# PixArt block on one core: nine narrow zero matmuls at the beginning, and each unit's third-next source transposed whole in beat 0, the turned maxima in a PSUM bank of their own

## The chip, the cores and the metric

One core of one Trainium2 chip. The metric is the time of one execution on the device in microseconds, the median of three runs. A profiled execution has a time of its own; its span runs from the first to the last profiled instruction.

## The reference

A PixArt transformer block for 16 batch items of 256 tokens, width 256, 16 heads of 16 values, in fp32: modulated self-attention, cross-attention to a context of 256 rows, and an MLP of width 1024. Cut to what matters:

```python
c_proj = jax.nn.silu(c) @ W_mod + b_mod
shift_a, scale_a, gate_a, shift_m, scale_m, gate_m = jnp.split(c_proj, 6, axis=-1)
x_norm = modulate(_ln(x), shift_a, scale_a)          # t * (1 + scale) + shift
q, k, v = jnp.split(x_norm @ W_qkv + b_qkv, 3, axis=-1)
attn_w = softmax(einsum('bhqd,bhkd->bhqk', q, k) * scale)
x = x + gate_a[:, None] * (einsum('bhqk,bhkd->bhqd', attn_w, v) @ W_proj + b_proj)
q_c = _ln(x) @ W_qc + b_qc
k_c, v_c = jnp.split(_ln(context) @ W_kvc + b_kvc, 2, axis=-1)
x = x + softmax(q_c k_c * scale) v_c @ W_cproj + b_cproj
x_norm2 = modulate(_ln(x), shift_m, scale_m)
x = x + gate_m[:, None] * (gelu(x_norm2 @ W_mlp1 + b_mlp1) @ W_mlp2 + b_mlp2)
```

## The kernel before

**Units and beats.** An attention of one kind (`s` self, `c` cross) for one batch item is a unit; there are 32, in the order s0 to s4, then alternately a new `s` and the `c` of an item whose `s` is done. The main loop calls `beat(n, k)` for n = -1 to 31 and k = 0 to 7. In a beat TensorE makes one eighth of the scores of the next unit (`s`, 4 matmuls, `s_tile`), one eighth of the transposed scores of this unit (`st`, 4 matmuls, `t_part`), and then something else: in even beats the weighted values of a finished quarter (`o`, 16 matmuls, `av_part`), in odd beats projections of coming units (`lanes`). VectorE takes the row maxima `mx` of each `s`, ScalarE the exponential `pt` of each `st`. After a beat all of `s` and `st` is written anew, so the next beat's `s` follows `mx` and its `st` follows `pt`.

**What a coming unit needs.** GpSimd normalises the source of unit n+4 in beat 4 or 5 of unit n and sets `ready`. One unit later it is unit n+3 (`q3` in `beat`): TensorE transposes it (`turn`, four transposes: two halves `f` of the width, each of two row tiles) into the PSUM tile `psT`, ScalarE and VectorE split it in beat 3 into a high and a low part (`xTh`, `xTl`), and K, V and Q follow by matmuls in beats 5, 7 and 1. K of the next but one unit ends in beat 7; in the next beat 0 ScalarE copies its high part (`h_k`, or `h_kc` for a cross unit), and VectorE, after this beat's `mx`, makes the low part (`l_k`, `l_kc`), each in two instructions, the last to read the tile `ps_k`.

**The turned maxima.** Half of a unit's row maxima are turned by one transpose in beat 4 of the unit before, half in beat 0 of its own (`m_turn`); ScalarE copies them negated (`m_row`) and a DMA puts them in as a further row of Q.

**PSUM.** Two double banks are held by `s` and `st`. One bank has the tag `gen` (LONG), and three have the tag `tr` (SHORT): `psT`, `ps_k`, `ps_q`, `o`, the maxima (`psm`) and others pass through these three. A new tile of a tag waits until a bank of the tag is released, that is, until all readers of its last tile are done.

**Order.** The text of the program sets the order on each engine (`InOrder`), so an engine that waits holds up all behind it. The beginning is a list of words, `PRE` in `E_` (line 55): `b9` is `busy(9, ...)`, nine matmuls of zeros into `s`; `brow` and `turn` transpose the biases and the conditioning (`c_sb`); `scale`, `shift` and `bq`, `bk`, `bv` are small matmuls; `T0t` transposes the first source; `Q0x0`, `Q0y0`, `Q0s0` send the first head group's parts of Q of unit 0 to their places by DMA from SP's queue, and a word ending in `0a` would use ScalarE's.

Of the kernel before, what the change touches and what calls it, by code (L numbers as in the profile page):

```python
# [16 lines left out]
P = 128  # L17
# [4 lines left out]
def pixart_block(  # L22
# [8 lines left out]
    B, N, H = x.shape  # L31
# [20 lines left out]
                return tc.keep_in_program_order(i) if self.on else i  # L52
            return issue

    E_ = {'M': ((-46, -37, -26, -24, -20, -20, -18), (-26, -17, -10, -8, 1, 1, 1), (-3, 1, 4, 7, 9, 9, 9), (8, 11, 13, 15)), 'LN': {'s': 'pool', 'c': 'pool', 'q': 'pool'}, 'ON': (1, 1, 1), 'H': (7, 11, 14, 15), 'AP': 23, 'DV': (1, 2), 'E': (-14, -6, -2, 2), 'HP': (1, 0, 2), 'W1P': [(-9, 3), (-8, 3), (-7, 3), (-6, 3), (-4, 5), (-4, 7), (-3, 1), (-3, 5)], 'W2P': [(-4, 3), (-4, 7), (-3, 2), (-3, 4), (-3, 6), (-3, 7), (-2, 0), (-2, 2), (-2, 4), (-2, 6), (-1, 0)], 'PRE': 'z0qp z0kp load ld2 ld3 rest L0a L0b silu b9 brow turn b1 L0f scale hik lok T0t shift b1 T0h T0l hiq one0a loq hiv bk K0a K0m L1a L1n lov L2a L2b bq K0h K0x K0y L1e K0l K0s Q0a Q0m Q0h Q0x0 Q0y0 T1t Q0l Q0s0 Q0r ldm T1h V0a V0b z1qa T1l bv L2c z1kp L3a L3b L3p L3c K1a K1b', 'SL': {(-1, 0): 'Q1a Q1b K1x K1y K1l K1s', (-1, 1): 'T2t T2h T2p V1a Q1x Q1y Q1l Q1s', (-1, 2): 'V1b rest', (-1, 3): 'rest z2ka', (-1, 4): 'M0 rest one1 ld4', (-1, 5): 'K2a vone', (-1, 6): 'K2m z2qa', (-1, 7): 'cpm2 c1 one2', (0, 0): 'cpm0 rest', (0, 1): 'rest', (0, 4): 'rest', (1, 0): 'rest', (1, 2): 'rest', (1, 4): 'rest'}}

    PE = InOrder(nc.tensor, True)
    ACT, DVE, POOL, SP = (InOrder(e, True) for e in (nc.scalar, nc.vector, nc.gpsimd, nc.sync))
# [122 lines left out]
    def busy(n, where):  # L181

        for _ in range(n):
            PE.matmul(where[:, :N], zw[:, :P], zw, start=True, stop=True)

    ts = [work.tile([P, 2, KC, H], F32, tag="pt", name=f"wf{i}", bufs=5) for i in range(3)]
    wm0, wm1, wk, wq, wv = (ts[i // 2][:, i % 2] for i in range(5))
# [540 lines left out]
    def m_turn(u, hf, pst=None):  # L728

        if pst is None:  # L730
            pst = ps_gen(f"psm_{u.n}_{hf}", SHORT)
        PE.transpose(pst[:16, :P], u.mx[:, hf].rearrange("p r a t -> p (r a t)"), ident)
        return pst
# [37 lines left out]
    def av_part(u, g):  # L771

        if g % 2 == 0:
            u.po = ps_gen(f"o_{u.n}_{g}", SHORT).rearrange("p (g n) -> p g n", g=2)
        for c in range(NT):
            for h in range(4):
                par, pair = h // 2, 2 * g + h % 2
                PE.matmul(u.po[h * 32:(h + 1) * 32, g % 2], u.v[:, c, par * 8 + pair], u.pt[pair][:, par, c],
                          start=(c == 0), stop=(c == NT - 1), tile_position=(0, h * 32))
        if g == 3:  # L780
            o_out(u, 1)
# [321 lines left out]
    def beat(n, k):  # L1103
        if n < 0:
            visit(n, k, (st, sp)[k % 2])
            return
        cur, prev, nxt = unit(n), unit(n - 1), unit(n + 1)
        q2, q3, q4 = (v if v and v.n >= m else None
                      for v, m in zip(map(unit, (n + 2, n + 3, n + 4)), (1, 2, 3)))
        p1, p2, p3 = (v and v.post for v in map(unit, (n - 1, n - 2, n - 3)))  # L1110
        alone = n > nu - 3
        lc = q4 if q4 and q4.kind == "c" else None
        ls = q4 if q4 and q4.kind == "s" else None
        lx = q3 if q3 and q3.kind == "c" else None
        late = lc and lc.b in (0, B - 1)
        if k == 0 and q2:
            q2.K.high()
            q2.K.send_high()
        if k == 2 and q2 and n:
            q2.V.keep()  # L1120
        if k == 4 and q2:
            q2.Q.high()
            q2.Q.send_high()
        if k == 6:
            if q2 and not n:
                q2.V.keep()
            if p2 and not alone:
                p2.end()
        kp = None
        if k == 5 and lx and n:  # L1130
            kp = lanes(q3.K, None if alone else p2)
        visit(n, k, between=kp and (lambda: run(kp, 2)))
        if k == 0:
            exps()
            if prev:
                av_part(prev, 3)
            if q3 and q3.ready:
                q3.T[0].place()
                pst = m_turn(cur, 1, q3.T[0].ps[:, N:])
                q3.T[0].turn((0,))  # L1140
            else:
                pst = m_turn(cur, 1)
            if prev:
                p1.pull_sums(1)
            m_row(cur, 1, pst)
            if q2:
                q2.K.low()
                q2.K.send_low()
            if p2:
                p2.norm()  # L1150
                p2.high()
                p2.low()
        elif k == 1:
            exps()
            run(lanes(q2 and q2.Q, q2 and n and q2.V))
            if prev:
                p1.pull_values(1)
            if lc:
                lc.ln[0].steps[0]()
            if lx:  # L1160
                if lx.b in (0, B - 1):
                    lx.ln[1].steps[0]()
                lx.ln[1].steps[1]()
                lx.ln[1].steps[2]()
        elif k == 2:
            exps()
            if cur:
                av_part(cur, 0)
            if q3:
                q3.T[0].turn((1,) if q3.ready else (0, 1))  # L1170
            if ls:
                ls.ln[0].steps[0]()
            elif prev:
                p1.recip()
                p1.spread()
            if not (q3 and q3.kind == "c"):
                spare(n)
        elif k == 3:
            if q3:
                q3.T[0].high()  # L1180
            exps()
            if q3 and q3.kind == "c" and n < nu - 4:
                q3.T[0].full()
            if alone and p2:
                p2.proj(0)
                p2.proj(1)
            elif n:
                run(lanes(p2, q2 and q2.Q))
            else:
                run(lanes(q2.V, q2.Q))  # L1190
            if q3 and q3.kind == "s":
                q3.T[0].low()
            if prev and ls:
                p1.recip()
                p1.spread()
            if lx and n == nu - 4:
                lx.T[0].parts[2]()
        elif k == 4:
            exps()
            if alone:  # L1200
                p2.end()
            if cur:
                av_part(cur, 1)
            if lx:
                lx.T[1].turn()
            if nxt:
                m_part(nxt, 0, st[:, 0] if lx else None)
            if q2:
                q2.Q.low()
                q2.Q.send_low()  # L1210
            if q3 and q3.kind == "c":
                if n < nu - 4:
                    q3.T[0].rest_pool()
                spare(n, not lc)
            if ls:
                ls.ln[0].steps[1]()
                ls.ln[0].steps[2]()
                ls.ready = True
        elif k == 5:
            exps()  # L1220
            run(kp or lanes(q3 and q3.K, (None if alone else p2) if n else q2.V))
            if cur:
                o_out(cur, 0)
            if lc:
                lc.ln[0].steps[1]()
                lc.ln[0].steps[2]()
                lc.ready = True
            if prev:
                p1.back()
            v = unit(n + 5)  # L1230
            if v and v.kind == "c":
                load(v)
        elif k == 6:
            exps()
            if lx:
                lx.T[1].high()
            if cur:
                cur.post.begin()
                av_part(cur, 2)
                cur.post.pull(0)  # L1240
            if q3 and p2:
                q3.vk = lanes(q3.V, q3.K)
                run(q3.vk, 1)
            if p3:
                p3.store()
            if lx:
                if lc:
                    p1.gate()
                    if not late:
                        lc.ln[1].steps[0]()  # L1250
        elif k == 7:
            exps()
            if lx:
                lx.T[1].parts[2]()
            run(q3.vk if q3 and p2 else lanes(q3 and q3.V, q3 and q3.K))
            if late:
                p2.add()
                p2.added = True
            elif lc and not lx:
                lc.ln[1].steps[0]()  # L1260
            v = unit(n + 5)
            if v and v.kind == "s":
                load(v)
            if n == nu - 1:
                p2.add()
                p2.store()
# [106 lines left out]
```

## Time and profile before

| | |
|---|---|
| time, median of 3 runs | 720.54 us (720.0 to 723.34) |
| profiled execution | 721.24 us, span 719.4 us |
| TensorE busy | 710.9 us, 99% of the span |
| VectorE, ScalarE, GpSimd busy | 79%, 77%, 73% |
| TensorE on the chain that ended last | 96% |

The names: PE is TensorE, PEld its weight loads, DVE VectorE, ACT ScalarE, POOL GpSimd, SP the queue that issues most DMAs. A row of the timeline has the start in us, the duration in us, the engine, the line, the operation, out<-in with the tiles' names, the shapes and a count; in brackets stands the engine's idle time before it and what ended it. All instructions are recorded by one helper and carry its line, L51, so the tile names tell them apart. A fp32 matmul that isn't of the rounded kind (`fp32r`) makes two passes on the array.

### The profile page before, as it was taken

Reading aid. Unit: us, or ns where it says so; the run is one execution under the profiler, and the core shown is the slowest. Engines: PE = TensorE matmul, PEld = TensorE weight load, DVE = VectorE, ACT = ScalarE, POOL = GpSimd, SP = SyncE. Lnnn points to the kernel's source line nnn. Section 1 sums busy time; section 2 is a strip of 40 time slices with the busy share of each in tenths; the row PEclk is TensorE's granted clock in tenths of the full one; section 3 lists DMA queues with packets and bytes.
Section 4 is the critical chain, followed back from the end, with each engine's and each line's share of the span. In section 5 each row is a group of like instructions: output and inputs, shape, how many; then the busy total and the mean of one; then the engine's idle time right before and its main releaser. Section 6 shows DMA issues by size and latency. Waiting matters only on the chain.

```text
span 719.4 us, 22486 instructions
## 1 busy us (share of the span) xinstructions
PE 710.9 (99%) x8991; PEld 591.3 (82%) x8991; DVE 565.9 (79%) x895; ACT 552.0 (77%) x955; POOL 521.7 (73%) x518
## 2 busy tenths in 40 slices
PE   9999999999999999999999999999999999999997
PEld 8777877778777787777877777787679999999997
DVE  4788888888888888888889888888765767777653
ACT  4677888888888888888888888878867677666761
POOL 6656678786866868686686788977866989666551
PEclk9999999999999999999999999999999999999999
DMA  6565445544545455454555656456322222313112
GB/s 209 193 218 185 153 163 180 179 164 166 186 139 193 157 185 187 165 180 136 196 165 188 204 171 198 148 196 195 105 73 97 76 68 80 80 55 88 53 52 74
DMA packets 81548, 106.15 MB, mean 148 GB/s; under 512 B 16610, under 2 KB 44548, under 8 KB 81444
## 3 DMA queue, kind: packets, MB, share of 16 engines
q1 hardware_dynamic: 80596, 104.43, 45.1%
q8 instruction: 71, 1.16, 0.7%
q10 hardware_dynamic: 848, 0.28, 0.2%
q14 instruction: 33, 0.27, 0.1%
HBM read 35.89 MB, written 8.98 MB: 62 GB/s over the span
## 4 chain that ended last, share of the span: by engine, by line
PE 96%; DVE 2%; issue 0%; ACT 0%; POOL 0%; ACTq 0%; POOLq 0%
PE s L51 19%; PE o L51 17%; PE st L51 16%; PE ph L51 12%; PE ps_qc L51 4%; PE ps_v_c L51 4%; PE ps_q L51 4%; PE ps_k L51 3%; PE ps_P_s L51 3%; PE ps_kc L51 3%; PE ps_v_s L51 3%; PE ps_P_c L51 2%; PE psT_c L51 2%; DVE mx L51 2%; PE psT_s L51 2%; PE psT_q L51 1%
## 5 line engine op out<-in xcount | busy, mean ns | idle before, releaser
L51 DVE TENSOR_REDUCE mx<-s 128x4 f32<-128x1024 f32 x252 | 307.9, 1222 | 72.5 <-PE s L51 68.8
L51 ACT ACTIVATE pt<-st 128x1024 f32<-128x1024 f32 x256 | 263.5, 1029 | 51.2 <-PE st L51 50.1
L51 PE MATMUL o<-pt,v 128*32 128x256 f32 x2048 | 137.0, 385 | 0.0
L51 PE MATMUL s<-big 63*128 63x256 f32 x1008 | 116.9, 306 | 1.1 <-DVE st_q L51 0.2
L51 PE MATMUL st<-big 64*128 64x256 f32 (+1 forms) x1040 | 107.6, 282 | 1.0 <-issue 0.6
L51 PE MATMUL ph<-xTh_m,wself 128*128 128x256 f32 x512 | 99.5, 280 | 0.0
L51 POOL TENSOR_TENSOR hl<-hf,hh 128x512 fp32r<-128x512 f32 x60 | 80.8, 1364 | 20.0 <-ACT hh L51 20.0
L51 PEld LDWEIGHTS s<-big 63*128 63x128 f32 x1008 | 77.3, 185 | 20.6 <-issue 7.5
L51 PEld LDWEIGHTS o<-pt,v 128*32 128x32 f32 x2048 | 53.4, 109 | 39.4 <-ACT oT L51 1.1
L51 PEld LDWEIGHTS st<-big 64*128 64x128 f32 (+1 forms) x1040 | 81.2, 186 | 3.9 <-ACT pt L51 1.5
L51 PEld LDWEIGHTS ph<-xTh_m,wself 128*128 128x128 f32 x512 | 82.0, 188 | 1.2 <-issue 0.4
L51 PE MATMUL ph<-xTl_m,wself 128*128 128x256 f32 x256 | 70.9, 277 | 0.0
L51 ACT ACTIVATE hf<-ph,bT 128x256 f32<-128x256 f32 x112 | 47.3, 476 | 21.1 <-PE ph L51 21.1
L51 ACT ACTIVATE hh<-ph,bT 128x256 fp32r<-128x256 f32 x112 | 47.3, 477 | 18.1 <-PE st L51 8.2
L51 PEld LDWEIGHTS ph<-xTl_m,wself 128*128 128x128 f32 x256 | 48.2, 188 | 0.0
L51 PE MATMUL s<-big,hh 128*128 128x256 f32 x256 | 45.2, 277 | 0.0
L51 DVE TENSOR_SCALAR xn_m<-x,mv_m,rs_m 128x256 f32<-128x256 f32 x28 | 33.5, 1236 | 14.8 <-POOL rs_m L51 14.8
L51 POOL TENSOR_SCALAR xn_q<-x,mv_q,rs_q 128x256 f32<-128x256 f32 x32 | 39.0, 1229 | 1.7
L51 POOL TENSOR_SCALAR xn_c<-c,mv_c,rs_c 128x256 f32<-128x256 f32 x32 | 39.0, 1229 | 1.7
L51 POOL TENSOR_SCALAR rs_c<-mv_c 128x2 f32<-128x2 f32 x16 | 3.7, 230 | 50.3 <-DVE mv_c L51 50.1
L51 PE MATMUL st<-big,hh 128*128 128x256 f32 x224 | 39.5, 276 | 0.0
L51 PEld LDWEIGHTS s<-big,hh 128*128 128x128 f32 x256 | 38.6, 188 | 0.0
(230 smaller groups left out, 2134.0 us busy)
## 6 DMA issues: line engine op xcount, KB each, us to landing
big<-h_k SPq DMA_DIRECT2D x32, 256.0 KB
big<-h_kc SPq DMA_DIRECT2D x32, 256.0 KB
big<-h_qc SPq DMA_DIRECT2D x32, 256.0 KB
big<-h_q SPq DMA_DIRECT2D x30, 256.0 KB
big<-l_k SPq DMA_DIRECT2D x16, 256.0 KB
g<-gd SPq DMA_DIRECT2D x16, 256.0 KB
U_s<-oT SPq DMA_DIRECT2D x32, 128.0 KB
R_s<-rd_s SPq DMA_DIRECT2D x16, 256.0 KB
```

The costliest lines, as they stand in the source:

```text
L51: i = f(*a, **k)
```

## The change

Four edits:

- `busy` multiplies zeros of 128 columns instead of 256. All its words are affected: nine at the very beginning, one before `shift`'s users, and one at the end of unit -1.
- The second word of zeros, after `turn`, is `b2` instead of `b1`: two narrow ones for one wide.
- `Q0y0` becomes `Q0y0a`: the send goes out from ScalarE's queue.
- In beat 0 of a unit with a source that is ready, the maxima get a tile `psm` of their own instead of the second half of `psT`, and the source's four transposes are all issued behind it; beat 2 then has none. Where the source is not ready (unit 0), all four stay in beat 2.

```diff
-    ... 'PRE': '... silu b9 brow turn b1 L0f scale ... Q0h Q0x0 Q0y0 T1t Q0l Q0s0 Q0r ...
+    ... 'PRE': '... silu b9 brow turn b2 L0f scale ... Q0h Q0x0 Q0y0a T1t Q0l Q0s0 Q0r ...
...
     def busy(n, where):
 
         for _ in range(n):
-            PE.matmul(where[:, :N], zw[:, :P], zw, start=True, stop=True)
+            PE.matmul(where[:, :P], zw[:, :P], zw[:, :P], start=True, stop=True)
...
             if prev:
                 av_part(prev, 3)
+            pst = m_turn(cur, 1)
             if q3 and q3.ready:
-                q3.T[0].place()
-                pst = m_turn(cur, 1, q3.T[0].ps[:, N:])
-                q3.T[0].turn((0,))
-            else:
-                pst = m_turn(cur, 1)
+                q3.T[0].turn()
             if prev:
                 p1.pull_sums(1)
             m_row(cur, 1, pst)
...
             if cur:
                 av_part(cur, 0)
-            if q3:
-                q3.T[0].turn((1,) if q3.ready else (0, 1))
+            if q3 and not q3.ready:
+                q3.T[0].turn()
```

How it moves the instructions, on TensorE, in beat 0 of unit 1, the first with a ready source; `o_2` is the end of the weighted values of unit 0, `mx` the maxima of unit 1, `xn_s` the normalised source of unit 4, `big` the Q and K of a unit, and in brackets stand the engines whose semaphores an instruction waits for. Before:

```order
L51 MATMUL psT_s_830<-ident,mx_527 16x128
L51 MATMUL psT_s_830<-ident,xn_s_692 128x128 [waits Pool_49] x2
L51 MATMUL s<-big_80 128x256 [waits DVE_49]
L51 MATMUL s<-big_80 128x256 x3
L51 MATMUL st<-big_78 128x256 [waits Activation_49]
L51 MATMUL st<-big_78 128x256 x3
L51 MATMUL ps_q_855<-xTh_s_620,wself 128x256 [waits DVE_49]
```

Now:

```order
L51 MATMUL psm_1_831<-ident,mx_528 16x128
L51 MATMUL psT_s_833<-ident,xn_s_693 128x128 [waits DVE_49,Pool_49]
L51 MATMUL psT_s_833<-ident,xn_s_693 128x128 [waits Pool_49]
L51 MATMUL psT_s_833<-ident,xn_s_693 128x128 x2
L51 MATMUL s<-big_80 128x256 x4
L51 MATMUL st<-big_78 128x256 [waits Activation_49]
L51 MATMUL st<-big_78 128x256 x3
L51 MATMUL ps_q_859<-xTh_s_621,wself 128x256 [waits Activation_49]
```

Four transposes stand where two stood. The first of them now waits for VectorE as well as for GpSimd, the `s` of beat 1 behind them has lost its wait for VectorE, and the first Q projection waits for ScalarE instead of VectorE.

On VectorE at the same place (`mx_813` are the maxima of unit 2, of which one instruction falls in beat 0 and the next in beat 1; `l_k` is the low part of K of unit 3):

```order
L51 TENSOR_REDUCE mx_528<-s 128x2x2 [waits PE_49] x3
L51 TENSOR_REDUCE mx_813<-s 128x2x2 [waits PE_49]
L51 TENSOR_SCALAR l_k_842<-ps_k_713,bqkv,h_k_805 128x256 [waits DMAHW3_49,Activation_49]
L51 TENSOR_SCALAR l_k_842<-ps_k_713,bqkv,h_k_805 128x256
L51 TENSOR_REDUCE mx_813<-s 128x2x2 [waits PE_49] x2
```

This is of the changed kernel; nothing moved here, the kernel before has the same rows under other buffer numbers.

On TensorE in beat 2 of the same unit, behind the weighted values `o`. Before:

```order
L51 MATMUL o_0_893<-pt_1_853,v_82 32x256
L51 MATMUL psT_s_830<-ident,xn_s_692 128x128 x2
L51 MATMUL s<-big_80 128x256 [waits DVE_49]
L51 MATMUL s<-big_80 128x256 x3
L51 MATMUL st<-big_78 128x256 [waits Activation_49]
```

Now:

```order
L51 MATMUL o_0_897<-pt_1_857,v_82 32x256
L51 MATMUL s<-big_80 128x256 [waits DVE_49]
L51 MATMUL s<-big_80 128x256 x3
L51 MATMUL st<-big_78 128x256 [waits Activation_49]
L51 MATMUL st<-big_78 128x256 x3
```

The two transposes are gone from here, and `s` of beat 3 follows `o` directly, with its wait for VectorE as before.

More of the change, by code (lines that the diff above doesn't have):

```diff
@@ L53, in __getattr__ @@
             return issue
-    E_ = {'M': ((-46, -37, -26, -24, -20, -20, -18), (-26, -17, -10, -8, 1, 1, 1), (-3, 1, 4, 7, 9, 9, 9), (8, 11, 13, 15)), 'LN': {'s': 'pool', 'c': 'pool', 'q': 'pool'}, 'ON': (1, 1, 1), 'H': (7, 11, 14, 15), 'AP': 23, 'DV': (1, 2), 'E': (-14, -6, -2, 2), 'HP': (1, 0, 2), 'W1P': [(-9, 3), (-8, 3), (-7, 3), (-6, 3), (-4, 5), (-4, 7), (-3, 1), (-3, 5)], 'W2P': [(-4, 3), (-4, 7), (-3, 2), (-3, 4), (-3, 6), (-3, 7), (-2, 0), (-2, 2), (-2, 4), (-2, 6), (-1, 0)], 'PRE': 'z0qp z0kp load ld2 ld3 rest L0a L0b silu b9 brow turn b1 L0f scale hik lok T0t shift b1 T0h T0l hiq one0a loq hiv bk K0a K0m L1a L1n lov L2a L2b bq K0h K0x K0y L1e K0l K0s Q0a Q0m Q0h Q0x0 Q0y0 T1t Q0l Q0s0 Q0r ldm T1h V0a V0b z1qa T1l bv L2c z1kp L3a L3b L3p L3c K1a K1b', 'SL': {(-1, 0): 'Q1a Q1b K1x K1y K1l K1s', (-1, 1): 'T2t T2h T2p V1a Q1x Q1y Q1l Q1s', (-1, 2): 'V1b rest', (-1, 3): 'rest z2ka', (-1, 4): 'M0 rest one1 ld4', (-1, 5): 'K2a vone', (-1, 6): 'K2m z2qa', (-1, 7): 'cpm2 c1 one2', (0, 0): 'cpm0 rest', (0, 1): 'rest', (0, 4): 'rest', (1, 0): 'rest', (1, 2): 'rest', (1, 4): 'rest'}}
+    E_ = {'M': ((-46, -37, -26, -24, -20, -20, -18), (-26, -17, -10, -8, 1, 1, 1), (-3, 1, 4, 7, 9, 9, 9), (8, 11, 13, 15)), 'LN': {'s': 'pool', 'c': 'pool', 'q': 'pool'}, 'ON': (1, 1, 1), 'H': (7, 11, 14, 15), 'AP': 23, 'DV': (1, 2), 'E': (-14, -6, -2, 2), 'HP': (1, 0, 2), 'W1P': [(-9, 3), (-8, 3), (-7, 3), (-6, 3), (-4, 5), (-4, 7), (-3, 1), (-3, 5)], 'W2P': [(-4, 3), (-4, 7), (-3, 2), (-3, 4), (-3, 6), (-3, 7), (-2, 0), (-2, 2), (-2, 4), (-2, 6), (-1, 0)], 'PRE': 'z0qp z0kp load ld2 ld3 rest L0a L0b silu b9 brow turn b2 L0f scale hik lok T0t shift b1 T0h T0l hiq one0a loq hiv bk K0a K0m L1a L1n lov L2a L2b bq K0h K0x K0y L1e K0l K0s Q0a Q0m Q0h Q0x0 Q0y0a T1t Q0l Q0s0 Q0r ldm T1h V0a V0b z1qa T1l bv L2c z1kp L3a L3b L3p L3c K1a K1b', 'SL': {(-1, 0): 'Q1a Q1b K1x K1y K1l K1s', (-1, 1): 'T2t T2h T2p V1a Q1x Q1y Q1l Q1s', (-1, 2): 'V1b rest', (-1, 3): 'rest z2ka', (-1, 4): 'M0 rest one1 ld4', (-1, 5): 'K2a vone', (-1, 6): 'K2m z2qa', (-1, 7): 'cpm2 c1 one2', (0, 0): 'cpm0 rest', (0, 1): 'rest', (0, 4): 'rest', (1, 0): 'rest', (1, 2): 'rest', (1, 4): 'rest'}}
     PE = InOrder(nc.tensor, True)
```

## The prediction

> **What bounds the kernel now.** I read the page first, for the engine that sets the end, then TensorE's waits, then the timeline of one unit at the beats that the change touches, then the first 21 us.
>
> ```profile
> span 719.4 us, 22486 instructions
> PE 710.9 (99%) x8991; PEld 591.3 (82%) x8991; DVE 565.9 (79%) x895; ACT 552.0 (77%) x955; POOL 521.7 (73%) x518
> PE 96%; DVE 2%; issue 0%; ACT 0%; POOL 0%; ACTq 0%; POOLq 0%
> ...
> PEld s L51 <- DVE mx L51: 5.2, 13, 0.6
> ```
>
> TensorE is busy 99% of the span and carries 96% of the chain that ended last. Its longest wait for another engine, the score matmuls `s` waiting for the row maxima `mx`, is 5.2 us in all. So time added to TensorE's stream, work or waiting, comes out at the end nearly one for one, and idle time of the others is free. The question for each edit is what it adds to or takes from that stream.
>
> The change acts in every unit whose third-next source was already normalised. In the kernel before, those are the units where the maxima are turned inside the `psT` bank:
>
> ```profile
> L51 PE MATMUL psT_s<-ident,mx x12: 276/277/278, 51.7 to 380.4; 128*16 128x128 f32 x12
> L51 PE MATMUL psT_c<-ident,mx x16: 276/277/278, 82.8 to 475.0; 128*16 128x128 f32 x16
> ```
>
> 12 + 16 = 28 units, from 51.7 to 475.0 us. Here is beat 0 of the first of them (start, duration, engine, operation; several rows of the timeline left out), and the same two instructions in the last one:
>
> ```profile
> 50.16 0.40 PE L51 MATMUL s<-big 63*128 63x256 f32 x4
> 50.36 0.85 ACT L51 ACTIVATE h_k<-ps_k,bqkv 128x256 fp32r<-128x256 f32 x2 [0.30 <-PE ps_k L51]
> 50.60 1.22 DVE L51 TENSOR_REDUCE mx<-s 128x4 f32<-128x1024 f32 x1 [0.64 <-PE s L51]
> 50.73 1.07 PE L51 MATMUL o<-pt,v 128*32 128x256 f32 x16
> 51.73 0.28 PE L51 MATMUL psT_s<-ident,mx 128*16 128x128 f32 x1
> 51.74 0.87 DVE L51 SCALAR_TENSOR_TENSOR l_k<-ps_k,bqkv,h_k 128x256 fp32r<-128x256 f32 x2
> 51.84 0.38 PE L51 MATMUL psT_s<-ident,xn_s 128*128 128x128 f32 x2
> 52.00 0.59 ACT L51 COPY oT<-o 128x512 f32<-128x512 f32 x1
> 52.15 0.51 PE L51 MATMUL s<-big 63*128 63x256 f32 x4
> ...
> 475.06 0.87 DVE L51 SCALAR_TENSOR_TENSOR l_kc<-ps_kc,bP,h_kc 128x256 fp32r<-128x256 f32 x2
> 475.16 0.38 PE L51 MATMUL psT_c<-ident,xn_c 128*128 128x128 f32 x2
> ```
>
> The reader is to see the order of events: TensorE reaches the source's transposes at 51.84, and VectorE finishes the pair `l_k` only at 51.74 + 0.87 = 52.61. At 475 us it is the same: 475.16 against 475.06 + 0.87 = 475.93. Before the change nothing ties the two together.
>
> **Beat 0: a new wait.** The short tag has three banks. At this moment one holds `o` (until the copy `oT`), one holds the K projection `ps_k` (until `l_k` has read it), and the third was free. The maxima now take the third, so the transposes must have a bank that is still in use, and the order shows which: their new wait is on VectorE, where in this beat `l_k` is the last reader of a short bank. `l_k` cannot come earlier: it stands behind `mx` (50.60 + 1.22 = 51.82), which stands behind this beat's `s`. How long TensorE takes from VectorE's end to its own start is seen in beat 4, where `s` does wait:
>
> ```profile
> 58.81 1.16 DVE L51 TENSOR_REDUCE mx<-s 128x4 f32<-128x1024 f32 x1
> 60.02 0.30 PEld L51 LDWEIGHTS s<-big 63*128 63x128 f32 x4 [0.34 <-DVE mx L51]
> 60.03 0.50 PE L51 MATMUL s<-big 63*128 63x256 f32 x4
> ```
>
> 58.81 + 1.16 = 59.97, and `s` starts at 60.03: 0.05 us. So the transposes start at 52.61 + 0.05 = 52.66 instead of 51.84, +0.82 us. Behind them on TensorE's queue stand `s` and `st` of beat 1 and the projections, with VectorE's next `mx` and ScalarE's next `pt` behind those.
>
> Four transposes run there instead of two. Unit 0 of the kernel before does four at once, right after `o`:
>
> ```profile
> 40.00 0.65 PE L51 MATMUL psT_s<-ident,xn_s 128*128 128x128 f32 x4
> ...
> 40.59 0.51 PE L51 MATMUL s<-big 63*128 63x256 f32 x4
> ```
>
> 0.59 us from the first to the next `s`; in beat 0 two take 52.15 - 51.84 = 0.31. So beat 1's `s` starts at 52.66 + 0.59 = 53.25 instead of 52.15: **+1.10 us**. Bounds: 0.77 + 0.23 = 1.00 with no signal time and only the difference between four transposes (0.59) and two (0.36, beat 2 below), both right after `o`; and 1.20 if the array, drained by the wait, costs another 0.1.
>
> [...]
>
> **Beat 2: two transposes leave.**
>
> ```profile
> 54.59 1.23 DVE L51 TENSOR_REDUCE mx<-s 128x4 f32<-128x1024 f32 x1 [0.67 <-PE s L51]
> 54.72 1.07 PE L51 MATMUL o<-pt,v 128*32 128x256 f32 x16
> 55.72 0.44 PE L51 MATMUL psT_s<-ident,xn_s 128*128 128x128 f32 x2
> 56.08 0.50 PE L51 MATMUL s<-big 63*128 63x256 f32 x4
> ```
>
> They hold TensorE from 55.72 to 56.08, 0.36 us. But the `s` behind them overwrites scores that `mx` reads until 54.59 + 1.23 = 55.82, so it can start at 55.87, not 55.72: **-0.21 us**, and -0.36 only if `mx` were no limit. The transposes' reader, the copy `xTh` in beat 3, gets its data earlier; ScalarE isn't the bound.
>
> **The maxima's own bank.** The transpose of the maxima is the same instruction in another bank and costs the same. Its reader, the copy `m`, stands behind `oT` on ScalarE (to 52.59), so an earlier release helps nobody. The first Q projection of beat 1 now takes the bank that `oT` frees at 52.59 and comes after 53.25: covered. It costs only if that cover goes.
>
> Per unit: 1.10 - 0.21 = 0.89 us, times 28 = **+24.9 us**. Bounds: 1.00 - 0.36 = 0.64, or 17.9 us; 1.20 - 0.15 = 1.05, or 29.4 us, where 0.15 leaves a little for a later `mx`.
>
> **The beginning.** Nine zero matmuls are issued as 18 passes, counted here as weight loads in two stretches, and what follows them:
>
> ```profile
> 1.17:5.17 4.00, 4.00 (x9) 3.19 (x10) 0.00 (x0) 1.00 0.79 223
> 5.17:7.20 2.03, 2.03 (x10) 1.54 (x8) 0.00 (x0) 1.00 0.96 287
> ...
> 4.29 0.41 DVE L51 SCALAR_TENSOR_TENSOR c_sb<-c_sb 16x256 f32<-16x256 f32 x1
> 5.97 0.16 DVE L51 SCALAR_TENSOR_TENSOR nb_s<-mv_s,rs_s 128x2 f32<-128x2 f32 x1 [1.27 <-POOL rs_s L51]
> 7.23 0.24 PE L51 MATMUL s<-ident,brow 32*128 32x32 f32 x1
> 7.79 0.60 ACT L51 ACTIVATE xn_s<-x,nb_s,rs_s 128x256 f32<-128x256 f32 x1
> 8.28 1.05 PE L51 MATMUL st<-sw,wf 128*128 128x128 f32 x8
> 9.17 0.60 PE L51 MATMUL psT_s<-ident,xn_s 128*128 128x128 f32 x4
> ```
>
> Ten passes take the first 4.00 us (0.40 each), eight the next 2.03 (0.25): TensorE starts slow and quickens at about 5 us, though the granted clock reads 1.00 in both. At half the columns a slow pass is 0.2 us, 18 of them 3.7 to 3.9 us, so they end at about 5.2 and the bias transpose starts there instead of 7.23, about 2 us sooner. What follows could use it: its other input `c_sb` is there at 4.70, the normalised source would be at 6.13 + 0.60 = 6.73 (ScalarE started it at 7.79 only behind copies that waited for TensorE), and the transposes of 9.17 would come at 7.2. I take **-1.9 us**. The later zeros, two narrow for one wide, are as many columns; the one narrow one before the Q bias hides behind VectorE. Bounds: 0, if weights not yet landed hold the next steps (the trace doesn't show single landings), and -2.1.
>
> [...]
>
> One send of Q's first head group moves from SP's queue to ScalarE's:
>
> ```profile
> 16.83 0.84 ACT L51 ACTIVATE xTh_s<-psT_s,sc 128x256 fp32r<-128x256 f32 x2
> 17.39 1.20 SPq L51 DMA_DIRECT2D big<-h_q  x2
> 18.68 0.54 SPq L51 DMA_DIRECT2D big<-l_q  x1
> 18.58 0.36 PE L51 MATMUL ps_k<-xTh_s,wself 128*128 128x256 f32 x1
> 20.86 0.50 PE L51 MATMUL st<-big 63*128 63x256 f32 x4 [0.62 <-issue]
> ```
>
> SP issues two sends in 1.20 us, so the third (`l_q`) goes out 0.6 earlier, and the first scores (20.86), which waited 0.62 for something the profile doesn't name, could come up to 0.6 earlier. Against that, the send stands before `xTh` on ScalarE, whose 0.6 us later end pushes K1 (18.58) by up to 0.4. Between -0.6 and +0.4 I take -0.2. The one narrow zero at the end of unit -1 saves at most 0.1.
>
> Sum: the profiled execution took 721.24 us (span 719.4 and 1.8 around it). 721.2 + 24.9 - 1.9 - 0.2 - 0.1 = 743.9. The median of the three runs, 720.54, lies 0.7 below the profiled one, so I predict **743.2 us**, 3.1% slower.
>
> **The rivals.** *Part of the wait is given back* (0.09): the added idle time lets VectorE and ScalarE get ahead, so that TensorE's later waits vanish. For: VectorE is at 79% only. Against: the waits of `s` for `mx` are loops within one beat, which a delay ahead of it shifts as a whole. If all 5.2 us went and the units cost the low bound of 17.9, it is 720.5 + 17.9 - 5.2 - 2.2 = 731; with half of that, and the units at the middle, up to 737.
>
> *Faster* (0.04): the wait is already met when TensorE gets there, because `o` or `st` in beat 0 come later than before relative to `mx`, or the bank is in fact another. It decides at 52.61: if TensorE reached the transposes 0.82 us later for another reason, the wait would cost nothing and one group of four would replace two of two: (0.31 + 0.36 - 0.59) x 28 = 2.2 us saved. With the beginning: 720.5 - 2.2 - 2.2 = 716. Against: 51.84 against 52.61 in the first unit and the same 0.77 in the last; nothing in the change moves `o`. About 0.02 more lies within 0.5%, which is about what a measurement of this kernel can tell from no change.
>
> *Dearer* (0.06): the restart after the wait costs more, or the three banks, now passed round among seven tenants a unit instead of six, add a second wait, at Q for `oT`. With 0.3 us more a unit, 8.4 us: 751 to 752. For: the wait for `oT` is new. Against: it ends 0.7 us before Q comes.
>
> *The beginning doesn't do it* (within the forecast): were the clock not opened by narrow zeros, the eight passes at 8.28 and those behind would run at half speed and eat about 1 us of the lead; 744 to 745.
>
> **How the numbers follow.** The forecast has 0.79. From the bounds its own range is 720.5 + 17.9 - 2.8 = 735.6 to 720.5 + 29.4 + 0.4 = 750.3; I write 735 to 750. That leaves out the faster case, no change, the dearer case and about half of the part given back: 0.04 + 0.02 + 0.06 + 0.05 = 0.17, so the range stays there. Faster by over 0.5%: 0.04; within: 0.02; slower: 0.94.
>
> **What would show it.** Right: in beat 0 a gap on TensorE ahead of the `psT` transposes of about 0.8 us, put down to `l_k` or `l_kc`, 28 times, some 23 us in all; beat 1's `s` about 1.1 us after where it was within the unit; in beat 2 `s` 0.05 after `mx`; the unit longer by 0.9 us; the first scores near 18.8 us. Wrong: no gap there, the transposes of beat 0 starting 0.11 us after the maxima's as before, or units of the old length.

## The result and the profile after

The changed kernel takes 744.78 us (median of six executions, 743.7 to 747.47) against 721.68 us for the kernel before, measured beside it (six executions): a ratio of 1.0326, 95% interval 1.0303 to 1.0348. It is slower by 3.3%; 743.2 was predicted.

The profiled execution took 747.47 us. The page of the changed kernel, its first rows and its chain; behind it the groups of TensorE's transposes (busy time, mean ns of one, then TensorE's idle time just before them and its releasers):

```profile
span 745.7 us, 22480 instructions
PE 714.3 (96%) x8993; PEld 594.6 (80%) x8993; DVE 569.3 (76%) x895; ACT 549.5 (74%) x955; POOL 520.4 (70%) x518
PE 63%; DVE 20%; POOL 7%; issue 6%; DMA 3%; ACT 1%; POOLq 0%; SPq 0%; ACTq 0%
```

```profile
L51 PE MATMUL psm<-ident,mx 128*16 128x128 f32 x48 | 13.3, 277 | 0.0
L51 PE MATMUL psT_s<-ident,xn_s 128*128 128x128 f32 x64 | 10.6, 290 | 8.8 <-DVE l_kc L51 4.3 <-POOL U_c L51 2.2 <-POOL xTh_ac L51 0.8
L51 PE MATMUL psT_c<-ident,xn_c 128*128 128x128 f32 x64 | 10.0, 280 | 12.0 <-DVE l_k L51 3.7 <-DVE l_kc L51 2.2 <-POOL xTh_as L51 2.2
```

TensorE works 3.4 us longer and the span is 26.3 us longer: the rest is idle time. It stands in front of the sources' transposes, 8.8 + 12.0 = 20.8 us there. Its share of the chain falls from 96% to 63%, and VectorE's rises from 2% to 20%.

The names behind the arrows need care. Only about half of the idle time is put down to `l_k` or `l_kc`; the rest goes to GpSimd's instructions. In the timeline they all look alike. Beats 0 to 3 of the first unit with a ready source, after the change (start, duration, several rows left out), and the same place in the last one:

```profile
49.95 1.23 DVE L51 TENSOR_REDUCE mx<-s 128x4 f32<-128x1024 f32 x1 [0.64 <-PE s L51]
50.08 1.07 PE L51 MATMUL o<-pt,v 128*32 128x256 f32 x16
51.08 0.28 PE L51 MATMUL psm<-ident,mx 128*16 128x128 f32 x1
51.10 0.87 DVE L51 SCALAR_TENSOR_TENSOR l_k<-ps_k,bqkv,h_k 128x256 fp32r<-128x256 f32 x2
51.35 0.59 ACT L51 COPY oT<-o 128x512 f32<-128x512 f32 x1
52.11 0.63 PE L51 MATMUL psT_s<-ident,xn_s 128*128 128x128 f32 x4 [0.75 <-DVE l_k L51]
52.67 0.51 PE L51 MATMUL s<-big 63*128 63x256 f32 x4
...
54.62 0.41 PE L51 MATMUL s<-big 63*128 63x256 f32 x4
55.08 1.23 DVE L51 TENSOR_REDUCE mx<-s 128x4 f32<-128x1024 f32 x1 [0.64 <-PE s L51]
55.20 1.07 PE L51 MATMUL o<-pt,v 128*32 128x256 f32 x16
56.36 0.51 PE L51 MATMUL s<-big 63*128 63x256 f32 x4
...
498.78 0.28 PE L51 MATMUL psm<-ident,mx 128*16 128x128 f32 x1
498.80 0.86 DVE L51 SCALAR_TENSOR_TENSOR l_kc<-ps_kc,bP,h_kc 128x256 fp32r<-128x256 f32 x2
499.81 0.63 PE L51 MATMUL psT_c<-ident,xn_c 128*128 128x128 f32 x4 [0.75 <-POOL x L51]
```

In the first unit `l_k` ends at 51.10 + 0.87 = 51.97 and the transposes start at 52.11. In the last, `l_kc` ends at 499.66 and they start at 499.81, again 0.15 later, though the row there names GpSimd's `x`. The order names VectorE as what they wait for in both, and in all 28 units the first transpose starts 147 or 148 ns after the pair `l_k` or `l_kc` ends, whatever name the row gives. So all 28 are the wait for the bank. From the maxima's transpose to the next `s` it is now 52.67 - 51.08 = 1.59 us, against 52.15 - 51.73 = 0.42 before.

From the first such unit to the last it is 498.78 - 51.08 = 447.70 us, against 475.04 - 51.73 = 423.31: 24.39 us over 27 units, **0.90 us each**. Twenty-eight make 25.3 of the 26.3 us.

The beginning, after the change (TensorE's rows; the first scores and the first product of the output at the end):

```profile
1.17 4.21 PE L51 MATMUL s<-zw 128*128 128x128 f32 x18 [1.17 <-DVE zw L51]
5.32 0.31 PE L51 MATMUL s<-ident,brow 32*128 32x32 f32 x1
5.90 1.22 PE L51 MATMUL s<-zw 128*128 128x128 f32 x4
6.92 1.92 PE L51 MATMUL st<-sw,wf 128*128 128x128 f32 x8
8.62 1.06 PE L51 MATMUL psT_s<-ident,xn_s 128*128 128x128 f32 x4
...
20.34 0.50 PE L51 MATMUL st<-big 63*128 63x256 f32 x4
38.35 1.07 PE L51 MATMUL o<-pt,v 128*32 128x256 f32 x16
```

The bias transpose starts at 5.32 instead of 7.23, the 1.9 us that were forecast. But the eight passes `st` behind it now take 1.92 us where they took 1.05, and the four transposes 1.06 where they took 0.60: slow passes. At the first `o` of the units only 39.00 - 38.35 = 0.65 us are left of the lead, in this execution.

### The profile page after: what moved, and what is told of

It reads as the page before. It is cut to its first block, busy times and chain, and to the rows that moved or that the text cites. A ratio compares the mean times of both kernels' runs of the same rounds, so it can differ in the third digit from the quotient of the medians.

```text
span 745.7 us, 22480 instructions
## 1 busy us (share of the span) xinstructions
PE 714.3 (96%) x8993; PEld 594.6 (80%) x8993; DVE 569.3 (76%) x895; ACT 549.5 (74%) x955; POOL 520.4 (70%) x518
## 3 DMA queue, kind: packets, MB, share of 16 engines
q8 instruction: 71, 1.16, 0.7%
## 4 chain that ended last, share of the span: by engine, by line
PE 63%; DVE 20%; POOL 7%; issue 6%; DMA 3%; ACT 1%; POOLq 0%; SPq 0%; ACTq 0%
PE s L51 15%; DVE mx L51 13%; PE ph L51 12%; PE st L51 11%; PE o L51 6%; PE ps_q L51 2%; PE ps_P_s L51 2%; PE ps_P_c L51 2%; PE ps_k L51 2%; DVE st_c L51 1%; PE ps_kc L51 1%; PE ps_v_s L51 1%; PE psT_s L51 1%; PE psT_c L51 1%; POOL xn_c L51 1%
```

## The experiments

My theory: in each unit TensorE stands still until `l_k` has read its bank, and that is nearly the whole loss. The rivals: four transposes at once cost it, whatever bank they have; or the beginning hides a larger loss or gain.

**The units' change alone.** The head stays as it was.

```diff
+            pst = m_turn(cur, 1)
             if q3 and q3.ready:
-                q3.T[0].place()
-                pst = m_turn(cur, 1, q3.T[0].ps[:, N:])
-                q3.T[0].turn((0,))
-            else:
-                pst = m_turn(cur, 1)
+                q3.T[0].turn()
...
-            if q3:
-                q3.T[0].turn((1,) if q3.ready else (0, 1))
+            if q3 and not q3.ready:
+                q3.T[0].turn()
```

> The kernel before with the change in the units alone (maxima in a bank of their own, all four transposes in beat 0); its beginning is that of the kernel before. Theory (a wait for l_k in each unit): in the changed kernel beat 1's s came 1.16 us later after the turned maxima than before, and beat 2 gave back some 0.25, so 28 x 0.91 = 25.5 us more than before, about 746 to 747 us, with the gap of 0.9 us in front of the transposes in 28 units. Rival (part of the loss lies in the beginning or in the end): clearly less than 24 us.

Measured: 747.76 us (745.5 to 750.2), ratio 1.0353 [1.0315, 1.0391]. The expectation was 746 to 747. In two of the four executions (749.39 and 750.2) the mean granted clock was 0.995, and the last section shows what that costs; the other two took 745.5 and 746.12, and the kernel before without such executions 721.1 in the median, so the units cost 24.7 us. The idle time in front of the sources' transposes is 9.0 + 12.0 = 21.0 us here, 0.75 a unit, where 0.9 was expected. So the units carry all of the loss, and the beginning takes a little off it.

**The beginning alone.** The units stay as they were.

```diff
-    ... 'PRE': '... silu b9 brow turn b1 L0f ... Q0x0 Q0y0 T1t ...
+    ... 'PRE': '... silu b9 brow turn b2 L0f ... Q0x0 Q0y0a T1t ...
-            PE.matmul(where[:, :N], zw[:, :P], zw, start=True, stop=True)
+            PE.matmul(where[:, :P], zw[:, :P], zw[:, :P], start=True, stop=True)
```

> The kernel before with the change at the beginning alone (narrow zeros, two for one, Q's send from ScalarE). Theory (the clock opens late after narrow zeros, as in the changed kernel's trace, where TensorE's passes stay at 0.21 us until 9.7 us): the lead of 1.9 us at the bias transpose shrinks to about 0.65 us at the first weighted values, so about 0.6 to 1.3 us under before. Rival (the late opening was an accident of that one execution, and the lead usually holds): 1.9 to 2.2 us under before, with passes of 0.11 us from about 5.3 us on.

Measured: 718.44 us (717.81 to 721.16) against 721.39 for before, ratio 0.9957 [0.9938, 0.9975]: a gain of 3.0 us, 1.8 to 4.5. That is more than either expectation gave (0.6 to 1.3, and 1.9 to 2.2). It is the fastest kernel of this study. Its profiled execution kept only 39.00 - 38.29 = 0.71 us at the first `o`, like the changed kernel's; why the time is better than that trace is taken up below, as far as it is known.

**The maxima in their own bank, the transposes still two and two.**

```diff
+            pst = m_turn(cur, 1)
             if q3 and q3.ready:
                 q3.T[0].place()
-                pst = m_turn(cur, 1, q3.T[0].ps[:, N:])
                 q3.T[0].turn((0,))
-            else:
-                pst = m_turn(cur, 1)
```

> As e1, but the transposes stay split as before, two in beat 0 and two in beat 2: only the bank of the maxima is changed. Theory (the loss is the bank, so the wait for l_k): the transposes of beat 0 wait 0.92 us more, beat 2 stays as before, 28 x 0.92 = 25.8 us more than before, about 747 us. Rival (the loss is in issuing four transposes at once in beat 0): about as before, 721 us.

Measured: 746.71 us (745.16 to 748.38), ratio 1.0338 [1.0303, 1.0374], as slow as with all four at once. Its first unit:

```profile
51.17 0.87 DVE L51 SCALAR_TENSOR_TENSOR l_k<-ps_k,bqkv,h_k 128x256 fp32r<-128x256 f32 x2
52.18 0.41 PE L51 MATMUL psT_s<-ident,xn_s 128*128 128x128 f32 x2 [0.74 <-DVE l_k L51]
52.52 0.51 PE L51 MATMUL s<-big 63*128 63x256 f32 x4
```

The same wait stands in front of two transposes. How many are issued together isn't the cause; the maxima's bank is.

**The maxima in their own bank, all four transposes in beat 2.**

```diff
-            if q3 and q3.ready:
-                q3.T[0].place()
-                pst = m_turn(cur, 1, q3.T[0].ps[:, N:])
-                q3.T[0].turn((0,))
-            else:
-                pst = m_turn(cur, 1)
+            pst = m_turn(cur, 1)
...
             if q3:
-                q3.T[0].turn((1,) if q3.ready else (0, 1))
+                q3.T[0].turn()
```

> As e1, but all four transposes are issued in beat 2, where l_k has long read its bank: the maxima have a bank of their own and the source is transposed whole. Theory (the loss is the wait alone): beat 0 loses two transposes (s 0.21 us sooner), beat 2 gets two (s 0.23 us later), so within 1.5 us of before, 720 to 723 us, and no wait for l_k. Rival (a seventh tile through three banks costs in any place): 10 us or more over before.

Measured: 728.25 us (726.41 to 729.71), ratio 1.0079 [1.0049, 1.0109]. A miss by some 5 us. The large wait is gone, as expected, but beat 0's saving comes back in beat 1. So the rival was right in kind, a further tile through three banks costs here too, though less than its 10 us. The groups of the first Q weights, for this kernel and then for the kernel before (two rows each), and one instance at 308 us:

```profile
L51 PEld LDWEIGHTS ps_q<-xTh_s,wself 64*128 64x128 f32 (+1 forms) x240 | 31.2, 190 | 2.5 <-DVE l_k L51 2.3
L51 PEld LDWEIGHTS ps_qc<-xTh_q,wqch 64*128 64x128 f32 x128 | 23.6, 185 | 3.1 <-DVE l_kc L51 3.1
```

```profile
L51 PEld LDWEIGHTS ps_q<-xTh_s,wself 64*128 64x128 f32 (+1 forms) x240 | 30.6, 185 | 0.1
L51 PEld LDWEIGHTS ps_qc<-xTh_q,wqch 64*128 64x128 f32 x128 | 23.6, 185 | 0.2 <-DVE l_kc L51 0.2
```

```profile
307.84 0.28 PE L51 MATMUL psm<-ident,mx 128*16 128x128 f32 x1
307.86 0.87 DVE L51 SCALAR_TENSOR_TENSOR l_k<-ps_k,bqkv,h_k 128x256 fp32r<-128x256 f32 x2
308.05 0.50 PE L51 MATMUL s<-big 63*128 63x256 f32 x4
308.78 0.18 PEld L51 LDWEIGHTS ps_q<-xTh_s,wself 64*128 64x128 f32 x1 [0.20 <-DVE l_k L51]
```

With the transposes gone from beat 0, `s` follows the maxima 0.21 us later instead of 0.42, and Q reaches its bank before `l_k` lets it go (307.86 + 0.87 = 308.73): 2.3 + 3.1 = 5.4 us of waits for `l_k` and `l_kc`, where the kernel before had 0.2. The bank is due at one time, and whoever asks for it first waits. (In its profiled execution, 727.9 us long, the clock was also halved for a while; that is the last section's.)

**The transposes ahead of the maxima.** The units' change alone, with the two statements of beat 0 in the other order.

```diff
-            pst = m_turn(cur, 1)
             if q3 and q3.ready:
                 q3.T[0].turn()
+            pst = m_turn(cur, 1)
```

> The units' change alone (the head as before), but with the source's four transposes written ahead of the maxima's turn in beat 0, so that the two trade the banks they are given: the transposes take the bank that came free earlier and it is now the maxima's turn that asks for the bank which `l_k` releases. Nothing is left out of the computation. Theory (the loss is TensorE standing idle until `l_k` has read its bank, and it shrinks by whatever is put in front of the waiting instruction): the four transposes, 0.56 us from their start to the first scores, now run while `l_k` is under way, and the wait of about 0.91 us shrinks to about 0.35 us in each of 28 units; 28 x 0.56 = 16 us less than the units' change alone, so about 732 us (729 to 736). Rival (the loss is four transposes in beat 0, or a wait that is as long wherever it stands): 746 to 749 us as before.

Measured: 734.27 us (733.29 to 738.92), ratio 1.0181 [1.014, 1.0221]; 13.5 us less than the units' change alone (12.3 without the executions at a mean clock of 0.995), where the theory said 16 and the rival nothing. The theory had taken a wait of 0.91 us, of which the trace shows 0.75 as idle time. The wait has moved to the maxima's transpose. What is left of it, as a group and in the first unit:

```profile
L51 PE MATMUL psm<-ident,mx 128*16 128x128 f32 x48 | 13.3, 277 | 7.8 <-DVE l_kc L51 4.2 <-DVE l_k L51 3.6
```

```profile
52.16 0.66 PE L51 MATMUL psT_s<-ident,xn_s 128*128 128x128 f32 x4
52.18 0.87 DVE L51 SCALAR_TENSOR_TENSOR l_k<-ps_k,bqkv,h_k 128x256 fp32r<-128x256 f32 x2
53.10 0.28 PE L51 MATMUL psm<-ident,mx 128*16 128x128 f32 x1 [0.28 <-DVE l_k L51]
```

7.8 us over 28 units is 0.28 each, against 21.0 with the units' change alone and 20.8 in the changed kernel. The instructions and the banks are the same; only useful work now stands in front of the wait. The idle time follows the bank and not the instruction: 20.8, 5.4 and 7.8 us for three tenants of it.

**How many narrow zeros.** Three kernels have the beginning alone, with 18, 13 and 6 narrow zeros in the first group in place of nine (`b18`, `b13`, `b6` for `b9`), and one repeats nine.

> The beginning alone (the units as before), with 18 narrow zeros in the first group in place of nine. Nothing is left out of the computation. If what opens the clock is how long TensorE is busy without a gap: 18 zeros of 128 columns at 0.21 us run to about 7.2 us, as long as nine of 256 columns did, the bias transpose starts at about 7.2 us, the full clock comes near 5 us as before, and the time is within 0.3% of the kernel before, 720 to 722 us. If narrow zeros never open it in time (the number of columns or of passes counts): the full clock comes at about 9.7 us, and the first output projection's product is no earlier or up to 1 us later than in the kernel before: 721 to 724 us.

> The beginning alone (the units as before), with 13 narrow zeros in the first group in place of nine. Nothing is left out of the computation. If what opens the clock is how long TensorE is busy without a gap, 13 zeros run to about 6.2 us, the full clock comes at about 5.2 us, the bias transpose starts at about 6.2 us with nearly all of the work behind it at full clock, and the lead of about 1 us is kept to the first scores: 718 to 720 us, at or below the beginning with nine narrow zeros (718.4). If narrow zeros do not open it: full clock at about 9.7 us, hardly any lead left at the first scores, 720 to 722 us.

> The beginning alone (the units as before), with six narrow zeros in the first group in place of nine. Nothing is left out of the computation. The six passes end about 0.64 us before nine do (3 x 0.213), so the bias transpose starts at about 4.7 us in place of 5.3, if its row has landed by then. [...] Rival (the number of zeros sets the opening): later than 9.8 us by as much as the zeros are fewer, 719 to 721 us.

> The beginning alone with nine narrow zeros once more, for its clock only. Nothing is left out of the computation. If the number of zeros sets the opening, the full clock comes at 9.7 to 9.8 us as in the two traces with nine narrow zeros so far. If the clock changes at boundaries 3.41 us apart whose place differs from one execution to the next, it comes either between 4.6 and 5.6 us (about one case in four or five) or anywhere between 8 and 12 us.

Measured: 18 zeros 723.21 us, ratio 1.0003 [0.9985, 1.0021]; 13 zeros 720.05, 0.9968 [0.9952, 0.9985]; six 721.24, 0.9993 [0.9974, 1.0012], a miss; nine once more, one execution, 719.71. Eighteen give the time of the kernel before, as the first theory said (with a reservation in the last section), and thirteen came out just above what it expected, which lies in the rival's range too. In their traces full clock came at 6.02 and 7.14 us, where the theory had it near 5, and the bias transposes at 7.68 and 7.02, where it had 7.2 and 6.2. With six nothing is gained: the condition that the expectation named, that the bias row has landed, isn't met. Full clock came at 9.59 us, before the 9.68 of the first trace with nine, where the rival had it later. First the timeline with six, then that of the repeat of nine:

```profile
1.17 2.93 PE L51 MATMUL s<-zw 128*128 128x128 f32 x12 [1.17 <-DVE zw L51]
5.13 0.28 PE L51 MATMUL s<-ident,brow 32*128 32x32 f32 x1 [1.03 <-DMA brow<-in_bias_rows_dram]
...
21.16 0.51 PE L51 MATMUL st<-big 63*128 63x256 f32 x4 [0.98 <-DMA big<-h_q]
```

```profile
5.31 0.31 PE L51 MATMUL s<-ident,brow 32*128 32x32 f32 x1
6.45 1.06 PE L51 MATMUL st<-sw,wf 128*128 128x128 f32 x8
7.34 0.60 PE L51 MATMUL psT_s<-ident,xn_s 128*128 128x128 f32 x4
...
36.66 1.07 PE L51 MATMUL o<-pt,v 128*32 128x256 f32 x16
```

With six, the bias row has not landed when the zeros end; the transpose waits 1.03 us for it and starts at 5.13, only 0.18 before that of nine zeros, and the first scores wait for a transfer of Q. Nine narrow zeros end just behind the row's landing. The repeat of nine is the same program as the beginning alone, and its passes `st` take 1.06 us where the first trace's were slow; it has 39.00 - 36.66 = **2.34 us** of lead at the first `o`, not 0.71. So the number of zeros alone doesn't set when full clock comes. It came at 5.87 us there, in neither of the two stretches that the other theory gave (4.6 to 5.6 and 8 to 12, my estimate), though 0.3 us from the first; the last section takes that up.

## Why the prediction was right, and where it was off

**The wait in beat 0 (+0.82 us): right in kind, a little small.** The transposes wait for `l_k` in all 28 units. The signal from VectorE's end took 52.11 - 51.97 = 0.14 us, where I had taken 0.05 from beat 4's `s`. The four transposes to `s` took 52.67 - 52.11 = 0.56, not 0.59, so the further 0.1 for a drained array, an estimate in the upper bound, doesn't show. In all beat 0 grew by 1.59 - 0.42 = 1.17 us, against 1.10. The gap was forecast at some 23 us in all and shows as 20.8, although the source's transposes start (52.11 - 51.08) - (51.84 - 51.73) = 0.92 us later: the page counts TensorE as busy for 0.28 us with the maxima's transpose, and idle only from there.

**Beat 2 (-0.21 us): as forecast.** From `o` to the next `s` it is 56.36 - 55.20 = 1.16 us, against 56.08 - 54.72 = 1.36: -0.20. The `s` starts 0.05 after `mx` ends (55.08 + 1.23 = 56.31); that wait is new, but it only limits the saving.

**Per unit 0.89, times 28 = 24.9:** measured 0.90, or 25.3. The longer beat 0 (+0.07) is nearly taken up by beat 1, about 0.05 shorter.

**The maxima's own bank "helps nobody", Q covered:** right here, and shown by what happens when the cover goes: with beat 0 short, Q waits 5.4 us for the same bank.

**The beginning (-1.9, with -0.2 for the send and -0.1 for the last zero):** the term of the sum that two traces contradict and a third confirms. The bias transpose came 1.91 us sooner; the 18 passes of the nine zeros (x18 in the row) took 5.32 - 1.17 = 4.15 us to it, more than the 3.7 to 3.9 of the estimate, which would have put it at 5.07 and not at the 5.2 that was used. That the steps behind narrow zeros run as fast as behind wide ones was my estimate; the first eight passes `st` took 1.92 and 1.91 us in two traces and 1.06 in the third, against 1.05 in the kernel before. The lead at the first `o` was 0.65 and 0.71 us in two traces with nine narrow zeros, and 2.34 in the third, with the units as before, where 2.2 was forecast; the first scores, forecast near 18.8 us, came at 20.34 in the changed kernel and at 18.65 in that third trace. The yardstick moves as well: three kernels with the old beginning reach the first `o` at 38.44 us (units alone), 38.40 (two and two) and 39.42 (transposes ahead), where the trace of the kernel before has 39.00. I had priced the late clock as a rival that depends on the kernel (were the clock "not opened by narrow zeros", about 1 us of the lead goes); it depends on the execution, and takes 2.34 - 0.71 = 1.6 us at the first `o` where it comes. To the end that difference doesn't last: the execution with the late clock took 719.45 us and the one with the early clock 719.71. Timed, the beginning gives 3.0 us alone (2.7 without the executions at a mean clock of 0.995 or less), more than any of the three traces' leads. Together with the units it is 747.76 - 744.78 = 3.0, but 745.8 - 744.78 = 1.0 against the two executions of the units alone at full clock; so there its worth lies open between 1 and 3 us. The send and the single later zeros were not tried by themselves.

**What is left.** The changed kernel's profiled execution is 745.7 - 719.4 = 26.3 us longer: 25.3 from the units, -0.65 from the head, and 1.65 that arises behind the units. Nothing shows that the 1.65 is the change's. VectorE's last row maxima of the units, at 520.0 us in the kernel before, come 24.9 us later with the units' change alone, and its span is 744.3 - 719.4 = 24.9 us longer: nothing arises behind the units there. With the units untouched, the repeat of nine zeros is 2.7 us ahead at that point and only 1.5 at the end, and the first trace of nine 1.1 ahead there and 1.8 at the end. So a microsecond or so in that last part differs without any change there; what makes it was not looked into. The profiled execution was also the slowest of the six, 2.7 us above their median.

The *faster* rival fell: the wait was met nowhere. *Part given back* fell too: 27 units kept 24.39 us. *Dearer* was right that a second tenant can be made to wait, but only in another kernel.

## What to carry over

When a tile gets a buffer of its own from a full pool, ask who holds that buffer now and who reads it last: the price is the time to that reader's end, once per turn (0.90 us a unit here), and in the order it shows as a changed releaser, not as a new instruction. If the bank can't be had earlier, put independent work in front of the instruction that asks for it (12 to 13 us here), and check the next tenant, which may wait in its place. A saving in the first microseconds should be judged by several executions, since full clock came at 5.87 us in one execution of a program and at 9.68 in another.

## What the runs showed of the hardware

The clock's full speed does not come at a fixed time after TensorE starts. The trace's record of the granted clock begins with its first change; the page's windows show 1.00 ahead of it too, so slow passes have to be read from their durations (the eight `st` at 6.92 in the changed kernel, 1.92 us at a printed 1.00). Full clock came at 5.20 us in the kernel before, and at 4.69, 4.54, 5.56 and 6.52 in the four others with nine wide zeros; with narrow zeros at 6.02 (18), 7.14 (13), 9.59 (six), and for nine at 9.83, 9.68 and 5.87, the last two in the same program.

Later the clock was halved for a time in three of the traces. The same stretch of the kernel before and of the one with six narrow zeros (busy time and instructions of PE, PEld, DVE, ACT and POOL, then the clock, the DMA share and GB/s):

```profile
36.90:43.70 6.80, 6.80 (x96) 5.53 (x96) 5.82 (x10) 4.72 (x8) 1.30 (x1) 1.00 0.58 188
36.90:43.70 6.80, 6.80 (x48) 4.97 (x46) 3.46 (x6) 2.05 (x2) 0.34 (x1) 0.50 0.59 199
```

TensorE is busy all through in both, and does 48 matmuls at half clock where it does 96 at full. The record gives 6.827 us of half clock here and the same in the two other traces (all transposes in beat 2, and 18 zeros), each time between 36.3 and 43.7 us. It begins 27.31 us after full clock was reached with six zeros, and 30.72 us after it in the other two. The 27.31 and 30.72 us are 8 and 9 times half of the 6.827, 3.413 us; the first stretch at full clock is 713.386 us in the kernel before and 733.866 in the changed one, 209 and 215 times. So these times from one change of the clock to the next are all whole multiples of 3.413 us, while the first change comes at another time in each execution.

What sets the first change is not shown. Nine wide zeros keep TensorE busy from 1.17 us to the bias transpose at 7.2, and with them full clock came between 4.5 and 6.5. Nine narrow ones end at 5.4, with the small bias transposes and a short stop behind them until 5.90; full clock came at 5.87 in one execution, and in the two others at 9.83 and 9.68, which is 3.41 us after 6.42 and 6.27. All three hold that small work, and by the windows TensorE is busy for 3.35 of the 3.41 us up to 5.87 in the first, and for 3.32 of those up to 6.42 and 6.27 in the others. So why full clock came some 4 us later there isn't shown. With six zeros the 3.41 us up to 6.18 hold the wait for the bias row, and TensorE is busy for only 2.3 of them; the clock rose at 9.59.

I don't know what halves the clock near 36 us. By half of 6.83 it should cost an execution 3.4 us, an estimate; the row maxima lag those of the kernel before by 0.1 us at 23 us and by 3.1 at 59 us with 18 zeros, by 0.3 and 3.1 with six, so about 3 us. The times agree: those of the kernel before with a mean granted clock of 0.995 or less took 723.6 to 726.2 us, the others 719.9 to 723.5. By this mark, the counts and the medians of the other executions are:

| kernel | at 0.995 or less | median of the others, us | kernel before beside it, the same way |
|---|---|---|---|
| kernel before | 15 of 57 | | |
| changed kernel | 0 of 6 | 744.8 | |
| units alone | 2 of 4 | 745.8 | 721.1 |
| beginning alone, nine zeros | 0 of 12 | 718.4 | 721.1 |
| two and two | 1 of 4 | 745.4 | 721.1 |
| all in beat 2 | 2 of 6 | 727.5 | 721.1 |
| transposes ahead | 1 of 4 | 733.5 | 721.9 |
| 18 zeros | 9 of 12 | 720.6 | 721.9 |
| 13 zeros | 1 of 12 | 719.9 | 721.9 |
| six zeros | 4 of 12 | 720.8 | 720.9 |

The losses of the units stand, and 2.7 of the 3.0 us of the beginning remain. With 18 zeros only three executions are left, so that this kernel equals the one before is in part a matter of these counts. Whether the zeros have a part in the counts was not tried.
